# Expert results scattered to their nodes' rows and loaded in groups, in place of gathers; another graph's scatters moved earlier

## The chip, the cores and the metric

The kernel is one program on one core of a Trainium2 chip. Its engines run side by side, each through its own instructions in order: PE (matrix products), DVE (vector work), ACT (functions and copies), POOL (here mostly the issue of indirect DMAs, which gather or scatter rows by a list of indices) and SP (plain DMAs). ACT's queue issues some plain DMAs too. The metric is the device time of one execution in microseconds (us).

## The reference

A network of four pairs of layers on 3125 nodes with 256 values each. Every layer is added to x, and every layer but the first input sees a layer norm of x:

```python
x = x + L0_gnn(norm(x))   # sum over 100000 weighted edges
x = x + L0_ffn(norm(x))   # 8 experts of 512, the best 2 of each node
x = x + L1_gnn(norm(x))   # graph attention, two layers, 50000 edges
x = x + L1_ffn(norm(x))   # 8 experts, the best 2
x = x + L2_gnn(norm(x))   # weighted graph convolution, then two dense layers
x = x + L2_ffn(norm(x))   # 4 experts; the choice comes from attention over another graph, 65536 edges
x = x + L3_gnn(norm(x))   # two mean convolutions
x = x + L3_ffn(norm(x))   # 8 experts of 1024, the best 2
```

Three of these, L0_ffn, L1_ffn and L3_ffn, are what this document calls expert rounds:

```python
topk_vals, topk_idx = top_k(xf @ Wg + bg, 2)
w = softmax(topk_vals)
for e in range(8):
    out += w_of(e)[:, None] * (act(xf @ W1[e] + b1[e]) @ W2[e] + b2[e])   # w_of(e) is 0 for nodes that didn't choose e
```

## The kernel before

Nodes lie in 25 tiles of 128 (the last holds 53); x stays in SBUF as `X`. Tiles are treated in six groups: five tiles four times, then four, then one (`GROUPS`). The program runs its steps in turn: `r0_gnn`, taking up of edges, then `middle` (`r0_ffn`, `r1_gnn`, `r1_ffn`, in which POOL keeps the order of the program text), `r2_gnn`, `r2_ffn`, `r3_gnn`, `r3_ffn`.

**An expert round.** While the layer before is still running, `mix_group` takes each finished group: norm, router, the two best experts of each node, and the node's place among the rows of each of the two. `mix_send` (L869) then has POOL scatter the normalised rows, one indirect DMA for a tile and a choice, into `regions`, a DRAM table with a stretch for each expert: 50 a round. Two row buffers hold the groups that wait for this. `gated` works on what was sent, in chunks of 256 rows of one expert. 28 chunks are always run; some more stand behind a branch that the data here does not take. For a chunk, SP reads the expert's number and the row from SBUF into registers and issues four loads (`gx_xs`, 256 KB of rows, L987; `gx_w1`, `gx_w2`, `gx_b2`). PE transposes the rows, DVE copies them (`gx_xt`, L999), PE computes the first layer (L1004), ACT applies the function (L1005), and PE the second layer (`second`, L974), one chunk behind the first. DVE adds the bias for each half of the chunk (L976) into `gx_ys`, and ACT's queue stores the chunk's 256 KB to `ff_results` in the order of the chunks (L977). The loop's tiles in SBUF have two buffers each.

**The collection.** When all chunks are done, the branch is passed (its `settle` reads one row of the other graph's table, `os_mark`, L1838), and `mix_result` gathers, for each tile and each of the two choices, 128 result rows of 1 KB with an indirect DMA on POOL (`gb_y`, L360) and adds them to `X` with their weights on DVE (L1035): 50 gathers and 50 additions a round. The first collection runs inside the start of `r1_gnn`, the second inside that of `r2_gnn`, mixed with norms and matrix products; the last is followed only by the stores of the output.

The plain DMAs of SP and ACT use eight semaphores in rotation, so that an issue waits for the DMA eight issues before it.

**The other graph.** The 65536 edges that `r2_ffn` needs are sorted by 512 scatters of 128 records each into `os_table` (`own_send`, L1826) on POOL. They depend on nothing but their records, and are spread over the earlier steps: 2 at each step of `r0_gnn`'s matrix loop (0 or 1 in its last part), each released by a step's ACT copy; 3 in each chunk of `r0_ffn`; 9 at each of four calls in the first attention layer of `r1_gnn` (`tail`); 3 or 4 in each chunk of `r1_ffn`; and what is left, 21, behind it, where `own_send()` stands between the first four gathers of the second collection and the others on POOL. In a chunk they stand ahead of the chunk's second layer.

## Time and profile before

| what | value |
|---|---|
| median of 10 runs | 5708.17 us (5701.96 to 5719.6) |
| the profiled execution | 5703.31 us |
| its span | 5701.4 us |
| mean granted clock of TensorE | 0.796 |
| busy of the span: PE, DVE, ACT, POOL | 64%, 50%, 38%, 37% |
| POOL: scatters to the other graph's table | 512, 551.1 us |
| POOL: scatters to the regions | 150, 148.3 us |
| POOL: gathers of results | 150, 153.4 us |

One profiled execution is shown as a page (busy times, the span in 40 slices, queues, the chain of work that ended last, the costliest groups of instructions), and its trace answers questions on a stretch, a tile or a line. In a line of a group, `a<-b` names what is written and read, `x150` counts; then come the busy time and the mean ns of one, and behind the second bar the time that the engine stood idle just before these instructions, with what ended most of it. `SPq` and `ACTq` are the queues' own instructions. A clock of 0.65 in a window is the mean of what the throttle granted in it. Stages lie in the span at: `r0_gnn` until about 780 us, `r0_ffn` 780 to 1005, the first collection and `r1_gnn` from there, `r1_ffn` 2840 to 3030, the second collection and `r2_gnn` from there, `r3_ffn` 5210 to 5630, the last collection to the end.

### The profile page before, as it was taken

To read this page: it belongs to the slowest core of one execution; us is meant where nothing else is said; L and a number is where in the kernel's file an instruction comes from. 1 tells how busy PE (TensorE), PEld (TensorE's weight loads), DVE (VectorE), ACT (ScalarE), POOL (GpSimd) and SP (SyncE) were. 2 spreads that over 40 slices of the span, in tenths; PEclk is the share of its full clock that TensorE was granted. 3 is DMA by queue.
4 is the path that set the end of the run, shared out by engine and by line. 5 is a ranking of instruction groups with operands and counts; after the bars stand their busy time and mean duration, and the time that the engine had idled before them with its cause. 6 is when DMAs were issued, how large, how long until landed. Compare 5 with 4: busy or idle time off the path is not lost. (4 is left out here: it accounts for less than half of the span.)

```text
span 5701.4 us, 66173 instructions
## 1 busy us (share of the span) xinstructions
PE 3631.1 (64%) x20909; PEld 2866.4 (50%) x20909; DVE 2854.3 (50%) x9396; ACT 2171.4 (38%) x5957; POOL 2108.9 (37%) x2107
## 2 busy tenths in 40 slices
PE   1499979324545324444573887554666699997994
PEld 1389858223333213333352676432433488886883
DVE  7978732434444335454524787524544787422112
ACT  2556432134554335445411797311222443111221
POOL 0766433455555455555357000245454000011003
PEclk9699979656666656666696998776777799997997
DMA  1722247333333133333163222211111011233554
GB/s 50 237 82 93 100 157 223 100 98 93 106 95 101 49 91 98 94 93 94 55 191 93 107 93 82 57 18 25 22 22 22 11 58 65 82 103 123 190 194 142
DMA packets 329439, 543.00 MB, mean 95 GB/s; under 512 B 69071, under 2 KB 242003, under 8 KB 325873
## 3 DMA queue, kind: packets, MB, share of 16 engines
q1 hardware_dynamic: 213430, 354.48, 18.9%
q0 software_dynamic: 84032, 154.27, 10.8%
q10 hardware_dynamic: 31610, 29.84, 1.6%
q8 instruction: 173, 2.83, 0.2%
q14 instruction: 194, 1.58, 0.1%
HBM read 393.49 MB, written 145.37 MB: 95 GB/s over the span
## 5 line engine op out<-in xcount | busy, mean ns | idle before, releaser
L360 POOL DMA_INDIRECT ad_rows<-r_rows,fa_gi x832 | 831.4, 999 | 632.9 <-PE ad_acc L2223 339.1
L1826 POOL DMA_INDIRECT os_table<-os_rec,os_at x512 | 551.1, 1076 | 637.9 <-ACT gx_h L1005 186.0
L360 POOL DMA_INDIRECT ad_rows<-q_rows,own_gi x416 | 399.8, 961 | 877.6 <-DVE ad_hb L2104 506.9
L2213 ACT ACTIVATE ad_rows<-ad_rows 128x64 f32<-128x64 f32 x2544 | 640.3, 335 | 149.0 <-issue 146.4
L2223 PE MATMUL ad_acc<-ad_rows,ad_hd 128*128 128x260 f32 x1664 | 601.1, 523 | 33.5 <-ACT ad_rows L2213 27.9
L2223 PEld LDWEIGHTS ad_acc<-ad_rows,ad_hd 128*128 128x128 f32 x1664 | 417.3, 265 | 122.3 <-ACT ad_rows L2213 35.7
L1654 PE MATMUL r_pa<-r_xs,r_cnt 128*128 128x257 bf16 (+1 forms) x3750 | 459.8, 276 | 11.9 <-issue 11.7
L869 POOL DMA_INDIRECT regions<-gh_xn,gd_at x150 | 148.3, 989 | 844.3 <-PE r_pa L1654 545.3
L1005 ACT ACTIVATE gx_h<-gx_pa,gx_bias 128x256 f32<-128x256 f32 x392 | 184.9, 473 | 607.3 <-PE gx_pa L1004 547.2
L1654 PEld LDWEIGHTS <-r_cnt 128*128 128x128 bf16 x3750 | 364.8, 99 | 67.6 <-issue 16.7
L1004 PE MATMUL gx_pa<-gx_xt,gx_w 128*128 128x256 f32 x1568 | 371.0, 392 | 22.7 <-DVE gx_xt L999 18.7
L974 PE MATMUL gx_po<-gx_w,gx_h 128*128 128x256 f32 x1568 | 370.5, 382 | 9.9 <-ACT gx_h L1005 6.8
L976 DVE TENSOR_TENSOR gx_ys<-gx_po,gx_b 128x256 f32<-128x256 f32 x168 | 70.5, 423 | 566.8 <-PE gx_po L974 491.8
L1004 PEld LDWEIGHTS gx_pa<-gx_xt,gx_w 128*128 128x128 f32 x1568 | 298.3, 195 | 89.1 <-DVE gx_xt L999 35.8
L360 POOL DMA_INDIRECT gb_y<-ff_results,gd_at x150 | 153.4, 1023 | 487.0 <-SPq L126 437.5
L974 PEld LDWEIGHTS gx_po<-gx_w,gx_h 128*128 128x128 f32 x1568 | 291.8, 191 | 52.3 <-ACT gx_h L1005 10.5
L1521 PE MATMUL r_pa<-r_xn,r_wt 128*128 128x257 f32 x1250 | 303.1, 387 | 17.6 <-ACT r_wt L1557 17.2
L2126 PE MATMUL ad_pt<-ident,ad_e 128*4 128x128 f32 x75 | 26.1, 348 | 452.0 <-DVE ad_e L2123 204.7
L2112 ACT CAST ad_hd<-ad_hb 128x2176 f32<-128x2176 bf16 (+1 forms) x50 | 98.3, 1967 | 566.0 <-PE ad_acc L2223 426.3
L2600 PE MATMUL ss_sum<-r_xw,ss_wt 128*128 128x256 f32 x1250 | 289.8, 394 | 6.4 <-DMA ss_wt<-mats 6.4
L2182 PE MATMUL ad_px<-ad_nb,ad_hT 128*128 128x24 bf16 x1248 | 45.3, 180 | 354.5 <-DVE ad_nb L1420 265.5
L2600 PEld LDWEIGHTS ss_sum<-r_xw,ss_wt 128*128 128x128 f32 x1250 | 245.6, 198 | 41.7 <-issue 6.8
(573 smaller groups left out, 7189.8 us busy)
## 6 DMA issues: line engine op xcount, KB each, us to landing
gx_w<-in_L_ffn_W SPq DMA_DIRECT2D x56, 1024.0 KB
mats<-r_wt SPq DMA_DIRECT2D x25, 1600.0 KB
ss_wt<-mats SPq DMA_DIRECT2D x25, 1600.0 KB
gx_w<-in_L_ffn_W SPq DMA_DIRECT2D x56, 512.0 KB
regions<-zero SPq DMA_DIRECT2D x26, 1024.0 KB
ad_rb<-fa_relT SPq DMA_DIRECT2D x48, 544.0 KB
gx_xs<-regions SPq DMA_DIRECT2D x84, 256.0 KB
ff_results<-gx_ys ACTq DMA_DIRECT2D x84, 256.0 KB
```

Of the source, the lines that this page charges most:

```text
L360: return self.nc.gpsimd.indirect_dma_start(out=out, out_offset=None, in_=table[:, :], in_offset=bass.IndirectOffsetOnAxis(ap=idx, axis=0))
L869: ins = nc.gpsimd.indirect_dma_start(out=self.regions[:, :], out_offset=bass.IndirectOffsetOnAxis(ap=m.at[i][:, t:t + 1], axis=0), in_=x, ...
L974: nc.tensor.matmul(po, h[:, f, j * P:(j + 1) * P], w2s[:, f, :], start=f == 0, stop=f == FC - 1)
L1004: nc.tensor.matmul(ps, w1s[:, c, f * P:(f + 1) * P], xt[:, c, :], start=c == 0, stop=c == DC - 1)
L1005: done = nc.scalar.activation(h[:, f, :], ps, act, bias=bias1[:, f, k:k + 1])
L1521: nc.tensor.matmul(pa, wt[:, i, :], xn[:, g * G + i, :], start=i == 0, stop=i == G - 1)
L1654: nc.tensor.matmul(pa[:, 0:n], c[:, u, :], xs[i][:, u, j, 0:n], start=u == 0 and j == 0, stop=u == T - 1 and j == 2)
L1826: i = nc.gpsimd.indirect_dma_start(out=s.table[:, :], out_offset=bass.IndirectOffsetOnAxis(ap=s.at[:, c:c + 1], axis=0), in_=s.rec[:, c, : ...
L2112: nc.scalar.copy(x.hd[:, :x.kb, :], x.hb[:, :x.kb, :])
L2213: i = nc.scalar.activation(v, v, AF.Copy, scale=x.rt[:, k, W4 + h:W4 + h + 1])
L2223: nc.tensor.matmul(x.acc, lhs[:, k, :], rhs[:, k, :], start=i == 0, stop=i == x.kb - 1)
L2600: nc.tensor.matmul(sums[t], wt[:, d, :], xw[:, d, :], start=d == 0, stop=d == T - 1)
```

## The change

A row in the regions gets one value more, a code: the node's number, plus 4096 times the number of its first choice, plus a tag of the round. The region table, its clearing, the row buffers and `gx_xs` are 257 values wide. `mix_group` computes the code with three more DVE operations a group.

In a chunk, `places` reads the code column of the 256 rows and computes with seven DVE operations on 128x2 values where each result goes: row node of `ff_results` if the chunk's expert is the node's first choice, row 4096 + node if it is not, and a row beyond the table, which is dropped, if the row holds no node of this round. `second` scatters each half of the chunk with an indirect DMA on POOL (56 a round), in place of ACT's store. `results` has a fixed size and is allocated once a round at its start; the padding rows are cleared by two DMAs, and the round's clearing of 1 MB goes, as do the operations at the start of `gated` that computed where to gather.

`mix_results` loads a group of tiles for one choice by one plain DMA on SP (12 a round, up to three groups ahead, four buffers) and keeps the 50 additions. `settle` reads one value of the results, which waits for all of the round's scatters; it is called ahead of the branch, at the end of its body and behind it.

`own_send` is spread otherwise: 3 in place of 2 at each step of `r0_gnn`'s loop, 7 in place of 9 in `tail`, 1 in place of 3 or 4 in each chunk of `r1_ffn`, after which nothing is left for the call behind it.

The diff, without the places where only a width or a name follows from the above:

```diff
-        self.regions = self.dram.tile([8 * RC, D], F32, name="regions")
+        self.regions = self.dram.tile([8 * RC, D + 1], F32, name="regions")
...
     def settle(self):
-        pass
+        if self.landing is not None:
+            self.nc.sync.dma_start(self.landed, self.landing[0:1, 0:1])
...
         with self.tc.If(cond):
             yield
+            self.settle()
...
+        m.tag = pool.tile([P, T], F32, name="gd_tag")
+        nc.gpsimd.iota(m.tag, pattern=[[P, T]], base=TAG * m.n, channel_multiplier=1, allow_small_or_imprecise_dtypes=True)
+        m.far = pool.tile([P, E], F32, name="gd_far")
+        nc.gpsimd.iota(m.far, pattern=[[HALF, E]], base=0, channel_multiplier=0, allow_small_or_imprecise_dtypes=True)
+        m.results = self.dram.tile([2 * HALF, D], F32, name=f"ff{m.n}_results")
...
+        e1 = hp.tile([P, TG, E], F32, name="gh_e1")[:, :G, :]
+        nc.vector.tensor_tensor(e1, s1, m.far[:, None, :].to_broadcast(all_), OP.mult)
+        nc.vector.tensor_reduce(rows[:, :, D], e1, AX.X, OP.add)
+        nc.vector.tensor_add(rows[:, :, D], rows[:, :, D], m.tag[:, gs])
...
-            adj = pool.tile([P, E], F32, name="gd_adj")
-            nc.vector.tensor_sub(adj, end, nch)
-            nc.vector.scalar_tensor_tensor(adj, adj, float(CH), zero, op0=OP.mult, op1=OP.subtract)
+            self.landing = results
             for i in range(2):
-                q = pool.tile([P, T, E], F32, name="gd_q")
-                nc.vector.tensor_tensor(q, sel[i], adj[:, None, :].to_broadcast([P, T, E]), OP.mult)
-                qs = pool.tile([P, T], F32, name="gd_qs")
-                nc.vector.tensor_reduce(qs, q, AX.X, OP.add)
-                nc.vector.tensor_add(pos[i], pos[i], qs)
-                nc.vector.tensor_scalar_min(at[i], pos[i], float(K * CH - 1))
-            results = self.dram.tile([K * CH, D], F32, name=f"ff{n}_results")
+                nc.scalar.dma_start(results[i * HALF + N:i * HALF + NP, :], self.zero[0:NP - N, 0:D])
...
                         nc.vector.tensor_add(y[:, j, :], po, b2s)
-                    nc.scalar.dma_start(results[k * CH:(k + 1) * CH, :].rearrange("(j p) d -> p j d", p=P), y)
+                        i = nc.gpsimd.indirect_dma_start(
+                            out=results[:, :], out_offset=bass.IndirectOffsetOnAxis(ap=to[:, j:j + 1], axis=0),
+                            in_=y[:, j, :], in_offset=None, bounds_check=2 * HALF - 1, oob_is_err=False)
+                        tc.declare_no_dep(i.ins, group=f"ff{m.n}_results", reason="nodes are distinct")
+                        tc.add_to_no_dep_group(f"ff{m.n}_results", i.ins)
+
+                def places(k, xs):
+                    code = xs[:, :, D]
+                    ci_ = yp.tile([P, CJ], I32, name="gx_ci")
+                    nc.vector.tensor_scalar(ci_, code, float(-TAG * m.n), None, op0=OP.add)
+                    old = yp.tile([P, CJ], F32, name="gx_old")
+                    nc.vector.tensor_scalar(old, code, float(TAG * m.n), 4.0 * HALF, op0=OP.is_lt, op1=OP.mult)
+                    e = yp.tile([P, CJ], I32, name="gx_e")
+                    nc.vector.tensor_scalar(e, ci_, 12, None, op0=OP.arith_shift_right)
+                    half = yp.tile([P, CJ], F32, name="gx_half")
+                    nc.vector.tensor_scalar(half, e, ek[:, k:k + 1], float(HALF), op0=OP.not_equal, op1=OP.mult)
+                    nc.vector.tensor_scalar(ci_, ci_, HALF - 1, None, op0=OP.bitwise_and)
+                    nc.vector.tensor_add(half, half, old)
+                    to = yp.tile([P, CJ], I32, name="gx_to")
+                    nc.vector.tensor_tensor(to, half, ci_, OP.add)
+                    return to
...
-                        xs = xp.tile([P, CJ, D], F32, name="gx_xs")
+                        xs = xp.tile([P, CJ, D + 1], F32, name="gx_xs")
...
                         nc.vector.tensor_copy(xt, pt)
+                        to = places(k, xs)
...
-                        if k == 3:
-
-                            nc.scalar.dma_start(results[KA * CH:K * CH, :].rearrange("(q p) d -> p q d", p=P),
-                                                self.zero[:, None, 0:D].to_broadcast([P, (K - KA) * CJ, D]))
...
                 with self.branch(n > KA):
                     chunks(KA, K)
-        m.results = results
+        self.settle()
+        self.landing = None
...
-    def mix_result(self, m, pool, t):
-
-        nc = self.nc
-        for i in range(2):
-            y = pool.tile([P, D], F32, name="gb_y")
-            self.gather(y, m.results, m.at[i][:, t:t + 1])
-            nc.vector.scalar_tensor_tensor(self.X[:, t, :], y, m.w[i][:, t:t + 1], self.X[:, t, :], op0=OP.mult, op1=OP.add)
+    def mix_results(self, m, pool):
+        nc, ys = self.nc, []
+        groups = list(GROUPS)
+        def fetch():
+            g, n = groups.pop(0)
+            y = pool.tile([P, 2, TG, D], F32, name="gb_y")
+            for i in range(2):
+                nc.sync.dma_start(y[:, i, 0:n, :], m.results[i * HALF + g * P:i * HALF + (g + n) * P, :].rearrange("(t p) d -> p t d", p=P))
+            ys.append(y)
+        for g, n in GROUPS:
+            while groups and len(ys) < 3:
+                fetch()
+            y = ys.pop(0)
+            for t in range(n):
+                for i in range(2):
+                    nc.vector.scalar_tensor_tensor(self.X[:, g + t, :], y[:, i, t, :], m.w[i][:, g + t:g + t + 1],
+                                                   self.X[:, g + t, :], op0=OP.mult, op1=OP.add)
+            yield g, n
...
-                    self.own_send(2 if g < T // G - 1 else src % 2, done)
+                    self.own_send(3 if g < T // G - 1 else src % 2, done)
...
     def settle(self):
+        super().settle()
         self.nc.sync.dma_start(self.o.mark, self.o.table[0:1, :])
...
             def tail(i):
-                self.own_send(9, i)
+                self.own_send(7, i)
...
-        self.gated(self.mix, "L1_ffn_w1", "L1_ffn_b1", "L1_ffn_w2", "L1_ffn_b2", AF.Gelu, send=3, more=2, tail=False)
+        self.gated(self.mix, "L1_ffn_w1", "L1_ffn_b1", "L1_ffn_w2", "L1_ffn_b2", AF.Gelu, send=1, tail=False)
```

## The prediction

> **What bounds the kernel now.** I read the page's costliest groups first, for the price of each operation that the change touches, then the windows, because the kernel is a row of stages with different limits, then who waits for the gathers, and last the chain.
>
> ```profile
> L1826 POOL DMA_INDIRECT os_table<-os_rec,os_at x512 | 551.1, 1076 | 637.9 <-ACT gx_h L1005 186.0
> L869 POOL DMA_INDIRECT regions<-gh_xn,gd_at x150 | 148.3, 989 | 844.3 <-PE r_pa L1654 545.3
> L976 DVE TENSOR_TENSOR gx_ys<-gx_po,gx_b 128x256 f32<-128x256 f32 x168 | 70.5, 423 | 566.8 <-PE gx_po L974 491.8
> L360 POOL DMA_INDIRECT gb_y<-ff_results,gd_at x150 | 153.4, 1023 | 487.0 <-SPq L126 437.5
> ```
>
> An indirect DMA holds POOL for about 0.97 us, whether it gathers or scatters, and the timeline adds 0.30 us of issue: 1.28 us each.
>
> The windows (columns: us, busy us and count of PE, PEld, DVE, ACT, POOL, then clock, DMA share, GB/s):
>
> ```profile
> 332.00:612.00 280.00, 275.38 (x1832) 250.56 (x1832) 232.25 (x599) 168.47 (x481) 167.31 (x159) 1.00 0.26 92
> 612.00:660.00 48.00, 47.88 (x300) 43.51 (x299) 42.90 (x159) 23.51 (x52) 6.55 (x7) 1.00 0.24 90
> 660.00:780.00 120.00, 76.08 (x389) 63.80 (x387) 65.61 (x324) 46.45 (x93) 55.54 (x56) 0.72 0.27 95
> 780.00:1005.00 225.00, 217.10 (x1029) 180.89 (x1029) 51.56 (x116) 55.01 (x113) 81.59 (x84) 0.98 0.71 219
> 1005.00:1120.00 115.00, 42.58 (x152) 30.82 (x152) 67.55 (x202) 25.59 (x63) 52.95 (x53) 0.65 0.37 101
> 2840.00:3030.00 190.00, 134.05 (x564) 100.34 (x564) 47.29 (x120) 28.48 (x58) 96.65 (x101) 0.90 0.60 176
> 3030.00:3065.00 35.00, 0.00 (x0) 0.00 (x0) 4.71 (x22) 0.23 (x1) 24.64 (x26) 0.51 0.21 46
> 3065.00:3165.00 100.00, 44.25 (x149) 32.32 (x150) 77.28 (x155) 26.91 (x67) 69.90 (x71) 0.68 0.24 63
> 5210.00:5630.00 420.00, 409.07 (x1911) 352.51 (x1910) 44.05 (x90) 106.01 (x224) 0.00 (x0) 0.98 0.56 184
> 5630.00:5702.00 72.00, 0.00 (x0) 0.00 (x0) 24.03 (x50) 0.00 (x0) 47.54 (x50) 0.50 0.46 137
> ```
>
> 332 to 660 is the first graph layer: PE is full, and POOL's 159 sends leave it idle for part of the time. 780, 2840 and 5210 begin the three expert rounds of 28 chunks: the first and third are PE's (217 of 225, 409 of 420), the second nobody's (PE 134 of 190). The windows that begin at 1005, 3030 with 3065, and 5630 are those in which results are collected: there PE stands at 0 to 44%. In the last, POOL's 50 gathers at 1.28 us are 64 us of the 72, while DVE has 24 us to do.
>
> ```profile
> L360 POOL DMA_INDIRECT gb_y<-ff_results,gd_at x150: 942/946/2159, 1007.0 to 5691.6; - x150
>   SPq L126: 437.5, 3
>   DMA gb_y<-ff_results,gd_at: 103.1, 70
> ```
>
> DVE waits 103 us for gathers, in 70 pieces. In the second collection the timeline shows why most: four gathers, then 21 sends in a row on POOL, then the next gather, while DVE stands still for 25 us:
>
> ```profile
> 3037.79 1.00 POOL L1826 DMA_INDIRECT os_table<-os_rec,os_at  x1 [0.30 <-issue]
> ...
> 3064.66 0.98 POOL L360 DMA_INDIRECT gb_y<-ff_results,gd_at  x1 [0.30 <-issue]
> ...
> 3067.60 0.48 DVE L1035 SCALAR_TENSOR_TENSOR X<-gb_y,gd_w,X 128x256 f32<-128x256 f32 x1 [24.97 <-DMA gb_y<-ff_results,gd_at]
> ```
>
> The end, from 5630, is one chain of gather, landing and DVE operation; a short and a long landing from it:
>
> ```profile
> 5657.73 2.47 DMA gb_y<-ff_results,gd_at
> ...
> 5677.81 4.19 DMA gb_y<-ff_results,gd_at
> ```
>
> **The change part by part**, against the profiled span of 5701.4 us (its execution 5703.3; the median of the runs is 4.9 us above that).
>
> *The end, from 5630.* 50 gathers go, 12 plain loads on SP take their place: 6.5 MB. In the first expert round the DMA engines reach 300 to 350 GB/s for stretches, so they need 19 to 22 us, against DVE's 24. Before: last add 5624.4, first gather 5630.1. After: the last scatter is issued at 5624.5, lands by 5628 (as the gathers' 2.5 to 4.2 us), then the new read that waits for it, the branch, and the read again, some 2.2 us each (the read of this kind that is there already took 2.1, from 3030.2 until SP went on at 3032.3): loads from about 5636, first group there at 5640, the last of DVE's 50 operations at 5665. From its last one to the end it was 5.8 us; I keep that: 5671, or −30. The four big output stores compete with the loads: 9.7 MB at 300 GB/s from 5636 end at 5668, so they fit. Ends: −35 (a faster settling) and −20 (loads at the 219 GB/s of the first round's mean, 30 us, with the stores behind).
>
> *The second collection, 3032 to 3165.* Off POOL: 50 gathers and 21 sends, 91 us; 25 additions of 0.83 us stay. What is late next is DVE: 4.7 + 77.3 = 82 us of work in 133. With 8 us until the first group is there and DVE nine tenths busy the stage lasts about 100: −33. Ends −45 (DVE without a gap) and −20 (only the 27 us of the sends, less settling).
>
> *The first collection, 1005 to 1120.* DVE has 68 us, and POOL's gathers run from 1007.0 to 1079.8. Loading hides that, but the next layer's first gather, at 1119.6, waits for normalisation, transposes and DVE work that stay; and the two reads cost some 4 us. I take −10, ends −20 and 0.
>
> *Tail of the first attention.* There the sends, 9 a call, run on POOL in two bursts of 18 without a pause (1910 to 1933, 1944 to 1967), and the next gathers start at once at 1967.6. 7 for 9 in the two calls of the later burst: 4 × 1.28 = −5.
>
> *The first graph layer.* 3 sends a step for 2 moves about 100 sends in front of 660. A step takes 3.5 us; 3 × 1.28 = 3.8 exceed it. From 332 to 612 POOL was idle between sends for 280 − 159 × 1.28 = 77 us, room for 60 of the extra ones; 40 remain at 612, 51 us of POOL. Until 660 there are another 39 us of room. So the first group's region scatters (661.8 to 674.7), which stand behind the sends in POOL's order, are 12 to 30 us late. Behind them waits the normalisation of the group after next, on ACT and DVE, since the rows have two buffers (ACT already waits 4.1 us for a region scatter). Later groups have pauses of 15 us between them, which take up part: +10, ends 0 and +25. PE's matmuls up to 660 do not wait for POOL.
>
> [...]
>
> *The chunk loops.* Each chunk gains two scatters on POOL (2.6 us, with the sends 6.4 us in the first round's 8.0 us chunk, 3.8 in the second's 6.8, 2.6 in the third's 15.0), seven tiny DVE operations (0.15 to 0.19 us, as the small ones in the trace, 1.2 us), and a row of 1028 bytes; it loses ACT's store and its place in the eight semaphore lanes that SP's loads wait for. The last tiny operation reuses a buffer that both scatters of two chunks ago read, so DVE now waits for their landing, and behind it stands the next chunk's bias addition. In the first and third round the landing (4 us) fits in the chunk: 0, ends −5 and +10. In the second the PE part is only 4.8 us and SP's six issues and their waits set the pace; the freed lane gains up to 0.5 us a chunk (SP's stalls there were 0.7), the wait costs up to 0.9: 0, ends −15 and +25. The rows of 1028 bytes: packets of 1040 bytes take 47 to 55 ns in this trace, of 1024 bytes 46, in loops that DMA does not bound: nothing.
>
> [...]
>
> *Small things.* Three more DVE operations per group (18 × 0.19 a round), about ten fewer at each round's start, two of them 128x200: +1. The zero fill of 1 MB becomes 150 KB: nothing, since it was hidden.
>
> Sum: −30 − 33 − 10 − 5 + 10 + 0 + 0 + 1 = −67. 5703.3 − 67 = 5636; with the 4.9 us to the median, 5641.
>
> **The rivals.**
> *Slower: the scatters' landing paces the loops.* If DVE's seven operations and the wait for both scatters fall on the path, each chunk pays 1.2 us plus some of the 2.5 to 4.2 us. It decides from 67 / 84 = 0.8 us a chunk over all rounds; at 1.2 us in all 84 it is +101, 5742. For it: the order on DVE puts the wait ahead of the addition that frees PE's output. Against: in 56 chunks DVE is busy under 25% and PE has two output buffers.
> *The backlog eats half.* Regions come 30 us late or more and the second round pays its 25: −67 + 15 + 25 = −27, 5681. For it: POOL's three sends exceed a step. Against: 39 us of room after 612.
> *More.* The second round was bound by lanes and POOL's 101 scatters, and loses 15 us or more, and the second collection gives 45: −67 − 15 − 12 = −94, 5614. For it: nobody is full there. Against: DMA is at 0.60.
> *The loads bring little,* because the two reads and the branch eat the early start and DVE was the next limit anyway: ends at −20, −20, 0: −34, 5674.
>
> **How the numbers follow.** Forecast 0.45, backlog 0.15, little from loads 0.12, more 0.10, landing paces 0.18, of which three quarters or so end slower. Its own range is 5625 to 5660. 0.2% (11 us) is about what a measurement tells from no change. Faster 0.81, same 0.05, slower 0.14. The range from 5600 to 5706 leaves out the worst of the landing case and a few in 100 below.
>
> **What would show it.** Right: no gathers after 5630 and the span's end 30 us after the first load; DVE without the 25 us wait after 3030; the regions' first scatter at 675 to 690; chunk loops of 225, 190 and 420 us as before. Wrong: DVE waiting for a scatter's landing at the line that computes the destinations, PE idle on the additions, the second loop over 200 us; or the first round starting 30 us late.

## The result and the profile after

The changed kernel takes 5748.72 us (median of 8 runs, 5741.27 to 5760.29) against 5706.28 us before (28 runs): a ratio of 1.0074, 95% interval 1.0065 to 1.0083. It is slower by 42 us where 67 us less were forecast, and outside the range. The profiled execution took 5743.91 us, its span 5742.0 us at a mean TensorE clock of 0.797 (before: 0.796).

Cut at the same instructions in both traces, the span goes as follows (us; the first stage ends with the last matrix product of `r0_gnn`'s loop, a round runs from its first transposition to its last bias addition, the attention from its first gather to its last):

| stage | before | after | difference | forecast |
|---|---|---|---|---|
| until the end of the first graph layer's loop | 737.9 | 878.7 | +140.8 | +10 |
| to the first expert round | 47.5 | 59.4 | +11.9 | 0 |
| first expert round | 217.2 | 244.9 | +27.7 | 0 |
| first collection | 117.0 | 93.3 | −23.7 | −10 |
| attention | 1621.5 | 1608.0 | −13.5 | −5 |
| to the second round | 110.9 | 109.8 | −1.1 | 0 |
| second round | 174.2 | 162.7 | −11.5 | 0 |
| second collection | 145.8 | 95.2 | −50.6 | −33 |
| to the third round | 2042.7 | 2039.5 | −3.2 | 0 |
| third round | 409.8 | 410.2 | +0.4 | 0 |
| end | 77.0 | 40.3 | −36.7 | −30 |
| sum | 5701.4 | 5742.0 | +40.6 | −68 |

(The forecast had 1 us more for small things.)

So the gains came, and were larger than forecast: the three collections gave 111 us where 73 were expected. What was forecast at +10 cost 141, and the first round 28 more. The 11.9 us between the loop and the first round belong to the rows of 257 values: every kernel here that has them takes 55 to 62 us there, every one with rows of 256 takes 47.5 to 51.6. Which part of it costs this was not taken apart.

The windows of after that answer to those of before (columns as there: us, busy us and count of PE, PEld, DVE, ACT, POOL, then clock, DMA share, GB/s):

```profile
332.00:612.00 280.00, 235.97 (x1362) 204.42 (x1363) 172.63 (x436) 132.72 (x372) 188.10 (x176) 0.90 0.20 71
612.00:740.00 128.00, 108.40 (x606) 91.13 (x605) 76.96 (x198) 55.97 (x162) 82.63 (x78) 0.90 0.20 71
740.00:880.00 140.00, 122.01 (x725) 107.55 (x723) 95.99 (x364) 58.56 (x129) 58.10 (x57) 0.93 0.29 104
935.00:1190.00 255.00, 224.10 (x1016) 184.54 (x1014) 67.12 (x304) 53.39 (x113) 136.11 (x140) 0.96 0.63 190
1190.00:1280.00 90.00, 37.79 (x152) 27.98 (x152) 66.80 (x202) 25.38 (x63) 3.31 (x7) 0.71 0.43 132
2985.00:3150.00 165.00, 125.64 (x547) 95.39 (x548) 64.15 (x294) 26.74 (x55) 74.83 (x77) 0.92 0.65 191
3150.00:3245.00 95.00, 44.78 (x167) 32.84 (x166) 77.89 (x190) 32.38 (x77) 26.07 (x31) 0.73 0.31 92
5702.00:5742.00 40.00, 0.00 (x0) 0.00 (x0) 19.97 (x50) 0.00 (x0) 0.97 (x1) 0.55 0.75 247
```

In the last line nothing but DVE and the loads is left of the end, and in the second collection (3150) POOL is down to 26 us and DVE at 78 of 95: both as the prediction says. The surprise is in the first two lines. From 332 to 612 PE was busy 275 of 280 us before, at full clock; now 236, at 0.90, though no matrix product of this stage waits for anything that POOL writes. And POOL, which was expected to be full, issued 176 operations in 280 us, only 17 more than before.

The groups of after that belong to this, from the page's costliest:

```profile
L1872 POOL DMA_INDIRECT os_table<-os_rec,os_at x512 | 550.7, 1076 | 628.9 <-ACT gx_h L1040 154.1
...
L888 POOL DMA_INDIRECT regions<-gh_xn,gd_at x150 | 148.2, 988 | 847.1 <-PE r_pa L1700 544.8
...
L1567 PE MATMUL r_pa<-r_xn,r_wt 128*128 128x257 f32 x1250 | 334.9, 414 | 87.9 <-ACT r_wt L1603 53.3
...
L990 POOL DMA_INDIRECT ff_results<-gx_ys,gx_to x168 | 163.5, 973 | 406.6 <-DVE gx_ys L989 373.7
```

The 168 scatters of results hold POOL 0.97 us each, the 150 gathers 1.02. The loop's matrix product r_pa has a mean of 414 ns and 88 us of idle time before it. By windows, before's group from 332 to 612 and after's from 332 to 740:

```profile
L1521 PE MATMUL r_pa<-r_xn,r_wt 128*128 128x257 f32 x785 | 184.4, 380 | 3.5 <-ACT r_wt L1557 3.1 <-issue 0.4
```

```profile
L1567 PE MATMUL r_pa<-r_xn,r_wt 128*128 128x257 f32 x843 | 227.3, 416 | 60.1 <-ACT r_wt L1603 30.2 <-ACT r_degs L1569 20.9 <-issue 8.2
```

The tile of collected results in after, and the end as the timeline shows it on SP and on DVE:

```profile
L1079 DVE SCALAR_TENSOR_TENSOR X<-gb_y,gd_w,X x150: 377/475/1023, 1198.3 to 5734.3; 128x256 f32<-128x256 f32 x150
L1070 SPq DMA_DIRECT2D gb_y<-ff_results x36: 332/1450/2487, 1191.6 to 5724.9; - x36
its engine sat idle before it (us, times) until:
  DMA gb_y<-ff_results: 15.0, 4
```

```profile
5706.76 2.15 SPq L112 DMA_DIRECT2D landed<-ff_results  x2
...
5709.45 15.91 SPq L1070 DMA_DIRECT2D gb_y<-ff_results  x12
```

```profile
5701.31 0.42 DVE L989 TENSOR_TENSOR gx_ys<-gx_po,gx_b 128x256 f32<-128x256 f32 x1 [3.03 <-PE gx_po L987]
5714.80 20.00 DVE L1079 SCALAR_TENSOR_TENSOR X<-gb_y,gd_w,X 128x256 f32<-128x256 f32 x50 [13.06 <-DMA gb_y<-ff_results]
```

DVE's wait for collected results fell from 103 us to 15. At the end, last bias addition, reads, loads and the first result addition follow in 13 us, and the 50 additions then run without a gap in 20.0 us.

PE's stalls in the first graph layer look like this in after's timeline (PE and ACT; a bracket gives the idle time before an instruction and what ended it):

```profile
703.82 0.97 POOL L1872 DMA_INDIRECT os_table<-os_rec,os_at  x1 [0.30 <-issue]
704.64 0.27 PE L1599 MATMUL r_pw<-r_hs,r_hd 128*128 128x128 f32 x1 [0.66 <-issue]
705.10 0.97 POOL L1872 DMA_INDIRECT os_table<-os_rec,os_at  x1 [0.30 <-issue]
705.38 0.27 PE L1599 MATMUL r_pw<-r_hs,r_hd 128*128 128x128 f32 x1 [0.47 <-issue]
706.09 1.12 PE L1567 MATMUL r_pa<-r_xn,r_wt 128*128 128x257 f32 x4 [0.45 <-issue]
...
709.64 0.81 PE L1567 MATMUL r_pa<-r_xn,r_wt 128*128 128x257 f32 x3 [1.20 <-issue]
711.09 0.27 PE L1599 MATMUL r_pw<-r_hs,r_hd 128*128 128x128 f32 x1 [0.64 <-issue]
```

In the middle of a row of matrix products whose operands are all there, PE pauses again and again for 0.3 to 1.2 us that the trace puts down to no wait at all ("issue"), while POOL issues one send after the other. POOL's row of sends ends at 709.9 (its next one starts at 714.27, after 4.38 us without one), and PE's last pause ends at 711.79.

### The profile page after: what moved, and what is told of

It reads as the page before. It is cut to its first block, busy times and chain, and to the rows that moved or that the text cites. A ratio compares the mean times of both kernels' runs of the same rounds, so it can differ in the third digit from the quotient of the medians.

```text
span 5742.0 us, 66747 instructions
## 1 busy us (share of the span) xinstructions
PE 3674.1 (64%) x20909; PEld 2889.5 (50%) x20909; DVE 2912.2 (51%) x10008; ACT 2169.5 (38%) x5957; POOL 2121.0 (37%) x2131
## 3 DMA queue, kind: packets, MB, share of 16 engines
q0 software_dynamic: 84896, 153.90, 10.4%
## 5 line engine op out<-in xcount | busy, mean ns | idle before, releaser
L1872 POOL DMA_INDIRECT os_table<-os_rec,os_at x512 | 550.7, 1076 | 628.9 <-ACT gx_h L1040 154.1
L1700 PE MATMUL r_pa<-r_xs,r_cnt 128*128 128x257 bf16 (+1 forms) x3750 | 458.8, 276 | 12.0 <-issue 11.9
L1567 PE MATMUL r_pa<-r_xn,r_wt 128*128 128x257 f32 x1250 | 334.9, 414 | 87.9 <-ACT r_wt L1603 53.3
L1567 PEld LDWEIGHTS r_pa<-r_xn,r_wt 128*128 128x128 f32 x1250 | 245.3, 207 | 137.8 <-ACT r_wt L1603 81.8
L990 POOL DMA_INDIRECT ff_results<-gx_ys,gx_to x168 | 163.5, 973 | 406.6 <-DVE gx_ys L989 373.7
L2643 PEld LDWEIGHTS ss_sum<-r_xw,ss_wt 128*128 128x128 f32 x1250 | 244.0, 197 | 40.6 <-issue 6.7
```

The costliest lines, as they stand in the source:

```text
L990: i = nc.gpsimd.indirect_dma_start(out=results[:, :], out_offset=bass.IndirectOffsetOnAxis(ap=to[:, j:j + 1], axis=0), in_=y[:, j, :], in_ ...
L1567: nc.tensor.matmul(pa, wt[:, i, :], xn[:, g * G + i, :], start=i == 0, stop=i == G - 1)
L1700: nc.tensor.matmul(pa[:, 0:n], c[:, u, :], xs[i][:, u, j, 0:n], start=u == 0 and j == 0, stop=u == T - 1 and j == 2)
L1872: i = nc.gpsimd.indirect_dma_start(out=s.table[:, :], out_offset=bass.IndirectOffsetOnAxis(ap=s.at[:, c:c + 1], axis=0), in_=s.rec[:, c, : ...
L2643: nc.tensor.matmul(sums[t], wt[:, d, :], xw[:, d, :], start=d == 0, stop=d == T - 1)
```

## The experiments

Two parts of the change were suspected of the first 141 us: the third send per step, and the rows of 1028 bytes, of which the regions' clearing has 26624. For the first round there was the prediction's own rival, the wait for the scatters' landing. The runs went to four chips. Those named with chip 1 and chip 4 met a before of 4867 and 4865 us, those with chip 5 and chip 6 one of 5694 to 5698 and 5646 us; the result above belongs with the second kind by its time. Each ratio below is against before on the same chip, and stages are compared within one kind of chip.

### Sends, clearing, buffers and the third send by itself, on chip 1

The changed kernel with the sends spread as before:

```diff
-                    self.own_send(3 if g < T // G - 1 else src % 2, done)
+                    self.own_send(2 if g < T // G - 1 else src % 2, done)
...
-                self.own_send(7, i)
+                self.own_send(9, i)
...
-  AF.Gelu, send=1, tail=False)
+  AF.Gelu, send=3, more=2, tail=False)
```

> The changed kernel with the sends spread as before (2 a step in the first graph layer, 9 in the attention's tail, 3 or 4 a chunk in the second round, 21 behind it). Theory: the third send a step keeps POOL running longer than a step and holds up PE; the loop of matrix products, which ran from 241 to 879 us in place of 241 to 738, ends some 85 us earlier, at about 795, and the rest of its delay, some 55 us, stays with the clearing. Against that the later places pay again: 13 us in the attention, 11 in the second round, 30 to 50 in the second collection, so 5690 to 5725 in all. Rival: the layer is late because of the clearing alone, the sends are hidden: the loop still ends at about 879, and the time is 5790 to 5820.

The changed kernel with the regions cleared in runs of 832 bytes instead of rows of 1028:

```diff
-        v = self.regions.rearrange("(q p r) d -> q p r d", p=P, r=8)
-        for q in range(v.shape[0]):
-            self.nc.sync.dma_start(v[q], self.zero[:, None, 0:D + 1].to_broadcast([P, 8, D + 1]))
+        v = self.regions.rearrange("(p r) d -> p (r d)", p=P).rearrange("p (c e) -> p c e", e=208)
+        for q in range(0, v.shape[1], 10):
+            n = min(10, v.shape[1] - q)
+            self.nc.sync.dma_start(v[:, q:q + n, :], self.zero[:, None, 0:208].to_broadcast([P, n, 208]))
```

> The changed kernel, the same bytes of the regions cleared in runs of 832 bytes, each at a multiple of 64 bytes, in place of rows of 1028. Theory: writes of 1028 bytes at addresses that are no multiple of 64 cost 94 ns a packet against 51 for 1024; with 832 aligned bytes a packet takes 40 to 50 ns, the clearing ends by 275 us as before, and the time falls by 45 to 60 us, to about 5695. Rival: the packets are slow since more traffic runs beside them; then 832 bytes take as long, and the time stays within 10 us of 5748.

The changed kernel with four buffers for the tiles of a chunk's results and destinations:

```diff
-tc.tile_pool(name="gx_y", bufs=2) as yp
+tc.tile_pool(name="gx_y", bufs=4) as yp
```

> The changed kernel with four buffers in place of two for the results and their destinations in the chunk loop, so that DVE waits for the scatters of four chunks ago. Theory: in the first round the wait for the landing goes (149 us of DVE's waits in 26 pieces), PE no longer waits for the additions, and the round takes 217 us as before in place of 245: the time falls by 25 to 30 us, to about 5720. Rival: the seven small DVE operations and the scatters on POOL themselves cost the 28 us: no change, within 8 us of 5748.

And the kernel before with the third send alone:

```diff
-                    self.own_send(2 if g < T // G - 1 else src % 2, done)
+                    self.own_send(3 if g < T // G - 1 else src % 2, done)
```

> The kernel before with 3 sends a step in the first graph layer and nothing else changed; what is sent there is missing from the end, so the second round sends fewer and nothing is left behind it. Theory: PE stalls as in the changed kernel, the loop of matrix products ends 70 to 100 us later than at 738; the second collection saves its 27 us and more: 5745 to 5780. Rival: the sends are hidden where POOL was idle: loop at 738 to 750, the time 5660 to 5685.

Measured, with stages in us:

| kernel | median | ratio and interval | loop ends | first round | second round | second collection |
|---|---|---|---|---|---|---|
| e1_sends_back | 4910.30 | 1.0093 (1.0077 to 1.0110) | 737.8 | 240.7 | 208.1 | 106.2 |
| e2_aligned | 4868.45 | 1.0002 (0.9992 to 1.0011) | 760.5 | 245.0 | 168.0 | 94.5 |
| e3_bufs4 | 4829.98 | 0.9928 (0.9911 to 0.9944) | 770.6 | 217.3 | 133.4 | 100.6 |
| e5_before_send3 | 4901.15 | 1.0070 (1.0054 to 1.0087) | 770.2 | 216.9 | 139.8 | 115.7 |

A run on chip 4 that sends and clears as fast as before does (e8_again, below) ends the loop at 700.1, so the third send costs 70 us of the loop here, and it does so as the prediction had described it: not by PE's stalls, but by the backlog on POOL. The windows of e5_before_send3:

```profile
332.00:612.00 280.00, 280.00 (x1862) 256.31 (x1861) 242.11 (x641) 166.54 (x472) 222.33 (x190) 1.00 0.27 97
612.00:700.00 88.00, 50.37 (x323) 45.37 (x321) 43.38 (x152) 25.81 (x56) 67.94 (x66) 0.81 0.16 52
```

and of e8_again, with two sends a step:

```profile
332.00:612.00 280.00, 280.00 (x1862) 256.30 (x1861) 241.78 (x641) 166.50 (x473) 165.00 (x159) 1.00 0.27 97
612.00:700.00 88.00, 84.05 (x520) 75.11 (x518) 69.76 (x266) 51.00 (x108) 36.24 (x36) 0.96 0.33 121
```

Until 612 PE is full in both, to the matrix product. But POOL got through 190 sends only: 222 us busy and 190 × 0.30 = 57 us of issue fill all of the 280. A send held it 1.17 us on average, with the issue 1.47, not 1.28; with two sends a step the mean was 1.04 (165.0 / 159). Why it rises is not shown. After 612 it had sends alone to do until the first scatter to the regions at 710.8 (645.5 in e8_again), and PE stands still for it once, in e5_before_send3's timeline:

```profile
730.41 1.22 PE L1521 MATMUL r_pa<-r_xn,r_wt 128*128 128x257 f32 x2 [67.81 <-ACT r_wt L1557]
```

That is ACT's copy queued behind a normalisation that waits for the regions' scatter (ACT's `gh_xn` waits for such scatters 4 times in that run, 82.3 us in all). Of the 70 us the second collection gave back 32 (147.6 to 115.7), and 34 stand in the total.

The landing wait is real in the first round, and four buffers remove it here: 245 to 217 us, which is before's time, and 168 to 133 in the second round. In after's first round the list of DVE's waits has

```profile
DVE gx_to L1010 <- DMA ff_results<-gx_ys,gx_to: 149.3, 26, 7.7
DVE gx_ys L989 <- PE gx_po L987: 7.6, 5, 4.5
```

(us in all, times, longest), and in e3_bufs4's the first line is gone; DVE now waits for the chunk's rows instead, in a round that PE fills:

```profile
DVE gx_ci L1000 <- DMA gx_xs<-regions: 115.0, 24, 5.7
DVE gx_ys L989 <- PE gx_po L987: 19.7, 22, 4.7
```

On this chip the change with four buffers is faster than before, with its three sends and its slow clearing.

### The same things on chip 5

The changed kernel again; the kernel before with the third send (the same kernel as e5_before_send3); the changed kernel with the aligned clearing (as e2_aligned); and all three repairs in one (aligned clearing, four buffers, sends as before).

> The changed kernel again, beside the runs that undo parts of it, since chips differ (on one the kernel before takes 5706 us, on another 4867). On the first: 1.0074 of the kernel before, the loop of the first graph layer ends at 879 us. On the second, from the runs that undo one part each: 4880 to 4920, 1.003 to 1.010 of the kernel before; the loop ends at 765 to 785 us without stalls of PE; the clearing's packets take 84 ns; the first round 245 us, the second 165 to 175.

> The kernel before with 3 sends a step in the first graph layer, again. On a chip on which the kernel before takes 5706 us: theory, PE stalls after some ten sends without a pause and the loop ends 70 to 100 us later than at 738 (5745 to 5780 in all); rival, the stalls of the changed kernel came from the clearing or the wide rows, and the loop ends at 738 to 775. On a chip like the last one: 1.007 again.

> The changed kernel with the clearing in aligned runs of 832 bytes and nothing else, on a chip of the kind on which the change was measured. Theory: the third send a step sets the first layer there, so the clearing is worth only the 20 us by which the changed kernel's loop (879) ends behind that of the kernel before with 3 sends (859): loop at 850 to 865, the time 15 to 25 us below the changed kernel's, 1.003 to 1.005 of the kernel before. Rival: its full length, 45 to 60 us: 0.996 to 0.999.

> The changed kernel with all three mended: aligned clearing, four buffers for results and destinations, sends spread as before. Theory: the loss in the first graph layer and the first round is gone and the gains in the collections stay: 1.5 to 2.3% faster than the kernel before on either chip (5575 to 5620, or 4755 to 4795). Rival: the second collection's gain came from having no sends behind the second round; then it is 0.8 to 1.2% faster at most.

| kernel | median | ratio and interval | loop ends | first round | second round | second collection |
|---|---|---|---|---|---|---|
| n_after | 5736.66 | 1.0078 (1.0053 to 1.0104) | 878.3 | 246.2 | 159.2 | 95.0 |
| e5_again | 5749.44 | 1.0096 (1.0064 to 1.0128) | 858.9 | 218.2 | 144.2 | 114.8 |
| f2_aligned | 5718.11 | 1.0034 (1.0019 to 1.0048) | 854.3 | 245.8 | 162.8 | 95.1 |
| e4_all | 5699.55 | 1.0004 (0.9990 to 1.0019) | 740.4 | 252.9 | 234.3 | 105.1 |

The result repeats. The third send alone moves the loop's end by 121 us (737.9 to 858.9), not by 70 as on chip 1. The aligned clearing takes 24 us off the changed kernel's loop (878.3 to 854.3). With both undone the loop is back at 740.4. The clearing itself, in after and then in f2_aligned (times of one issue, minimum, median and maximum in ns, and first and last start):

```profile
L104 SPq DMA_DIRECT2D regions<-zero x26: 539/5398/6810, 182.5 to 309.8; - x26
```

```profile
L105 SPq DMA_DIRECT2D regions<-zero x26: 372/3293/4148, 182.3 to 260.4; - x26
```

Before's last one starts at 264.7. Of the packets in the trace, those of 1028 bytes took 94 ns on average, before's of 1024 bytes 51 ns, f2_aligned's of 832 bytes 44 ns. PE feels it: from 180 to 332 it is busy 57 us in after and 92 in before, and one copy r_wt of ACT waits 20.3 us, until 334.8, for a store of the matrices that SP issued behind the clearing, at 323.3. On chip 1, where the sends do not stall PE, e1_sends_back shows the clearing by itself: its loop ends at 737.8, e8_again's on chip 4 at 700.1.

How far the loop is at a given time tells where its delay arises. It has 1250 products r_pa; the ends of three of them, in us:

| kernel | chip | 125th | 1125th | 1250th |
|---|---|---|---|---|
| before | of the result | 291.4 | 659.5 | 737.9 |
| after | of the result | 345.7 | 807.4 | 878.7 |
| e5_again | 5 | 318.9 | 780.2 | 858.9 |
| f2_aligned | 5 | 288.7 | 783.3 | 854.3 |
| e8_again | 4 | 292.7 | 643.4 | 700.1 |
| e5_before_send3 | 1 | 292.3 | 643.5 | 770.2 |

On the result's kind of chip the whole delay is there by the 1125th product, and the first scatter to the regions follows it within 3 us (809.6 in after, 782.5 in e5_again), as in before (661.8): POOL's backlog has no part in it. On chip 1 nothing is lost by the 1125th, and all 70 us come after it, in the wait for the regions. So the third send costs the loop on both kinds of chip, but in two different ways.

e4_all shows the other side. With the sends back in the rounds and four buffers, the loop is repaired, but the second round takes 234 us: here POOL has 3 or 4 sends and two scatters a chunk. And the first round, which four buffers had brought to 217 us on chip 1, stays at 253.

### Where the sends can go, on chip 5

e7_mix is e4_all with 2 or 3 sends in turn at a step and 2 a chunk in the second round:

```diff
-                    self.own_send(2 if g < T // G - 1 else src % 2, done)
+                    self.own_send(2 + src % 2 if g < T // G - 1 else src % 2, done)
...
-  AF.Gelu, send=3, more=2, tail=False)
+  AF.Gelu, send=2, tail=False)
```

> As the last, with the sends spread in between: 2 and 3 by turns in the first graph layer, 9 in the tail, 2 a chunk in the second round, 15 behind it. Theory: 2.5 x 1.28 = 3.2 us fits in a step of 3.5, so the loop ends as before, and the second round loses less to sends than with 3 or 4: 0 to 15 us faster than the run with all three mended. Rival: what counts is that POOL pauses within a step; then the loop stalls or regions come late, and it is slower than that run by 20 us or more.

5709.63 us, 1.0025 (1.0014 to 1.0037): loop 792.9, first round 251.9, second round 194.5. Half of a third send is half of the cost (52 us), and the second round gets shorter with fewer sends (234.3 us with 3 or 4 a chunk, 194.5 with 2). f1_nosend0 is e4_all without the 84 sends of the first round, which then go behind the second:

```diff
-beside=self.fill_edges, send=3, tail=False
+beside=self.fill_edges, send=0, tail=False
```

> All three mended (aligned clearing, four buffers, sends as before), and no sends in the first round: its 84 are sent behind the second round, so only the first round is to be read. Theory: five indirect DMAs a chunk (6.4 us of POOL in 7.5) hold up the first round on chips of this kind, not the scatters of results as such; with two a chunk it takes 215 to 222 us as before the change, in place of 246 to 253. Rival: the new scheme itself (the wait for landing, the small operations on DVE) costs the 30 us: 240 or more.

One run, 5772.83 us, with the first round at 220.2 us: on this kind of chip, with four buffers, it is the sends beside the scatters that lengthen the round, and not the new scheme as such. With them POOL has 5 indirect DMAs in a chunk of 7.75 us (217 / 28), at 1.28 us each 6.4 of it. Two a chunk cost nothing, as in the third round, which takes 410 us with its 56 scatters and without. How five of them hold up the round is open: in e4_all's first round PE's 25 us of idle time all stand before instructions that carry a wait. The 84 sends behind the second round made that collection 189 us.

### What in a third send stops PE

Four variants of before. Three have one thing more at each of the 100 steps of the loop's four full groups: m1_poolwork adds POOL arithmetic of 0.77 us, m2_hwdma a small plain DMA on SP, and f4_few an indirect DMA of 16 single values to a table that nobody reads:

```diff
+                    if g < T // G - 1:
+                        x = nc.gpsimd.tensor_add(scr, scr, scr)
```

```diff
+                    if g < T // G - 1:
+                        x = nc.sync.dma_start(extra[g * T + src], self.o.rec[:, g * T + src, :])
```

```diff
+                    if g < T // G - 1:
+                        x = nc.gpsimd.indirect_dma_start(
+                            out=extra[:, :], out_offset=bass.IndirectOffsetOnAxis(ap=few[0:16, g * T + src:g * T + src + 1], axis=0),
+                            in_=scr[0:16, 0:1], in_offset=None, bounds_check=1600 - 1, oob_is_err=False)
```

m4_burst leaves the number of sends and puts them in rows of ten:

```diff
-                    self.own_send(2 if g < T // G - 1 else src % 2, done)
+                    self.own_send((10 if src % G == G - 1 else 0) if g < T // G - 1 else src % 2, done)
```

> The kernel before, with one addition of 128x288 on POOL more at each step of the first graph layer (100 of about 0.9 us, released like a send), so POOL is as busy as with 3 sends but issues no more DMAs; the output is the same. On a chip on which the kernel before takes some 5700 us: theory, PE is held up by the issue of indirect DMAs without a pause; the additions are hidden in POOL's idle time, the loop still ends at 738 to 765 us. [...] On a chip on which it takes some 4870 us: hidden, at most 10 us.

> The kernel before, with one plain DMA on SP more at each step of the first graph layer that writes 128 records of 4 bytes to a scratch table (100 in all, released like a send), so the DMA engines get the small writes of a third send while POOL issues none of them; the output is the same. Theory: what holds PE up is POOL's issuing, so the loop ends at 738 to 760. Rival: the small writes or their completions hold PE up: 820 to 870.

> The kernel before with the same number of sends in the first graph layer, but 10 at each fifth step in place of 2 at each. Theory: PE stalls when POOL has issued some ten indirect DMAs without a pause, so ten at once and 4 us of pause stay near that limit: loop at 738 to 770. Rival A, it is the number of sends that counts: 738 to 745. Rival B, what counts is any stretch in which POOL issues without a pause: later than 770.

> The kernel before with one indirect DMA of 16 records (in place of 128) more at each step of the first graph layer, to a scratch table; the output is the same. It takes POOL nearly the same issue as a whole send. Theory: what holds PE up is the number of indirect DMAs that POOL issues without a pause, so the loop ends at 820 to 860 as with 3 whole sends. Rival: it is the small writes, an eighth here: 740 to 765.

| kernel | chip | median | ratio and interval | loop ends |
|---|---|---|---|---|
| m1_poolwork | 6 | 5646.95 | 1.0002 (0.9985 to 1.0019) | 741.5 |
| m2_hwdma | 6 | 5676.69 | 1.0053 (1.0039 to 1.0068) | 764.0 |
| m4_burst | 6 | 5657.17 | 1.0014 (1.0002 to 1.0027) | 746.5 |
| f4_few | 5 | 5809.35 | 1.0195 (1.0169 to 1.0222) | 869.8 |

POOL's time is not the price: 76 such additions between 332 and 612, 59 us, cost nothing, though POOL is busy 243 of the 280 us there and only 188 in after. Nor are bytes or the table's random rows: 100 indirect DMAs of 64 bytes each cost the loop 132 us (869.8 against before's 737.9), somewhat more than 100 sends (121). Rows of ten sends alone cost little. Each indirect DMA beyond two a step costs the loop 1.0 to 1.3 us on these chips (52 us for 50 in e7_mix, 121 for 100 in e5_again, 132 for 100 in f4_few). The groups of f4_few between 332 and 740 (columns as in the page's groups; several releasers are given):

```profile
L1528 PE MATMUL r_pa<-r_xn,r_wt 128*128 128x257 f32 x852 | 226.7, 411 | 27.9 <-ACT r_wt L1564 14.0 <-issue 13.0
...
L1560 PE MATMUL r_pw<-r_hs,r_hd 128*128 128x128 f32 x851 | 123.3, 289 | 25.1 <-issue 20.9 <-DVE r_hs L1551 1.9 <-DVE r_hd L1556 1.9
```

More than half of the idle time before PE's matrix products ends with no wait. Sorted by whether the matrix product or its weight load carries a wait, and counted within the window from the modelled end of one to the start of the next, PE's idle time is:

| kernel | chip | window | at a wait, us | without one, us |
|---|---|---|---|---|
| before | of the result | 332 to 612 | 4.1 | 0.5 |
| after | of the result | 332 to 740 | 41.1 | 22.5 |
| e5_again | 5 | 332 to 740 | 55.8 | 19.2 |
| f4_few | 5 | 332 to 740 | 27.4 | 35.5 |
| m4_burst | 6 | 332 to 612 | 6.7 | 7.6 |
| m1_poolwork | 6 | 332 to 612 | 10.4 | 0.0 |
| e5_before_send3 | 1 | 332 to 640 | 0.0 | 0.0 |

The pauses without a wait stand at the end of long rows. Take as a row the indirect DMAs that POOL starts with less than 0.45 us between one and the next: of after's 40 such pauses of over 0.15 us, 38 begin at or behind the ninth DMA of a row, in f4_few 49 of 52, and in m4_burst all 15 between 332 and 612 at the tenth and last or just behind it. This is what m4_burst's expectation called the limit of some ten, and why its rows of ten cost little: each loses only its end. On chip 1 POOL runs on from 332 to 612 and PE has no such pause.

The waits are mostly for ACT's copy r_wt. That it comes late because PE's products before it were late is an inference; no run separates the two. In after the loop's rate falls from 785 products r_pa in 280 us (2.80 per us) to 843 in 408 (2.07), which is 107 us: 59 from PE's idle time (64 of 408 us instead of 5 of 280), and the other 49 from longer products, 416 ns instead of 380 for r_pa, at a granted clock of 0.90 instead of 1.00.

DVE is slower beside POOL's arithmetic: from 332 to 612 DVE's r_hd takes 486 ns in m1_poolwork and 366 in before. It is hidden all the same, since DVE at 274 of 280 us stays beside PE; and it is not what the sends do, beside which r_hd takes 366 ns in e5_again too.

### The part that pays, without the sends

e8_hybrid keeps 257 values a row (cleared in runs of 832 bytes) but uses the new scheme, scatters and group loads, in the third round only; the first two rounds store, gather and send as before. Its core, where `place` is true in the third round:

```diff
+        place = m.n == 3
...
-                        i = nc.gpsimd.indirect_dma_start(
+                        if not place:
+                            continue
+                        i = nc.gpsimd.indirect_dma_start(
...
+                    if not place:
+                        nc.scalar.dma_start(results[to * CH:(to + 1) * CH, :].rearrange("(j p) d -> p j d", p=P), y)
```

> Rows of 257 values with an aligned clearing, sends as in the kernel before, results scattered and loaded in the third round only (28 chunks of 15 us, 2 scatters each); the first two rounds store by chunk and gather as before. Theory: the gain of the last collection (77 us to 40) stays and nothing is lost: 5655 to 5675 where the kernel before takes 5700, 4825 to 4835 where it takes 4867, 0.992 to 0.9945 of it. Rival: the wider rows cost in the other places: 0.997 to 1.000.

On chip 6 5617.64 us against 5645.73, a ratio of 0.9944 (0.9925 to 0.9964): faster than before, where the changed kernel has 1.0074 and 1.0078. Loop 728.8, first round 217.6, second round 166.1, end 39.8. What the change brings at the end it keeps.

e9_hybrid4 adds one send a chunk in its second round, so that none is left behind it:

```diff
-  AF.Gelu, send=3, more=2, tail=False)
+  AF.Gelu, send=4, more=2, tail=False)
```

> The kernel with the new scheme in the third round alone, with 4 or 5 sends in each chunk of the second round in place of 3 or 4, so that none is left behind it. Theory: a send there costs some 0.4 us of the round (174 us with 98, 144 with about 20), and the 21 behind it 27 us of the collection: 12 to 20 us faster than with 3 or 4, 0.990 to 0.993 of the kernel before. Rival: more than four indirect DMAs a chunk hold up PE, the round takes 25 us longer, and nothing is won.

5660.69 us on chip 5, 0.9940 (0.9918 to 0.9962). The collection is 32 us shorter than e8_hybrid's (147.6 to 115.6) and the round 35 longer (166.1 to 201.5): nothing won. e10_late21 moves the call for the 21 left sends behind the collection in the program's text:

```diff
         self.gated(self.mix, "L1_ffn_w1", ..., send=3, more=2, tail=False)
-        self.own_send()
...
+            self.own_send()
             self.own_load()
```

> The same kernel as e8_hybrid, for the chip of this call, beside e10. Both theories: 28 us below before (0.994 to 0.996), second round 166 to 175 us, collection behind it 146 to 148 us, with DVE's wait of some 25 us behind the 21 sends.

> As e8_hybrid, but the 21 sends that are left stand behind the second collection's 50 gathers instead of behind its first four. Theory that DVE's 25 us wait for a gather queued behind the sends is time on the path: the collection's additions end some 20 us earlier, and of that 0 to 20 us are lost again where the other graph's table is read 27 us later; 10 to 20 us below e8_hybrid (0.9965 to 0.9985 of it, 0.990 to 0.992 of before). Rival, that POOL's 71 indirect DMAs in a row set the collection whatever their order: the same time as e8_hybrid, with the stage from the last addition of the second round to the first sums of the third layer at 146 to 148 us.

On chip 4 e8_again takes 4828.21 us, 0.9926 (0.9909 to 0.9943), and e10_late21 4825.46, 0.9919 (0.9903 to 0.9936): no difference between the two that these runs can tell. The edit did less than its expectation supposed: the scheduler put the sends among the gathers, from 2506.6 to 2571.0, and not behind the last. The gathers and result additions of the first two rounds in e8_again:

```profile
L369 POOL DMA_INDIRECT gb_y<-ff_rows,gd_at x100: 942/946/2265, 976.5 to 2583.4; - x100
L1092 DVE SCALAR_TENSOR_TENSOR X<-gb_y,gd_w,X x100: 437/479/1099, 981.2 to 2590.8; 128x256 f32<-128x256 f32 x100
```

and in e10_late21:

```profile
L369 POOL DMA_INDIRECT gb_y<-ff_rows,gd_at x100: 942/947/2262, 976.7 to 2584.7; - x100
L1092 DVE SCALAR_TENSOR_TENSOR X<-gb_y,gd_w,X x100: 444/480/1277, 981.3 to 2595.2; 128x256 f32<-128x256 f32 x100
```

The additions of the second collection begin 27 us earlier (2480.8 in place of 2507.9), yet the last gather starts 1 us later and the last addition 4 us later; the stage takes 148.6 us in place of 147.6. The list of DVE's waits between 2470 and 2600 has for e8_again

```profile
DVE X L1092 <- DMA gb_y<-ff_rows,gd_at: 40.3, 17, 24.0
```

and for e10_late21

```profile
DVE X L1092 <- DMA gb_y<-ff_rows,gd_at: 48.0, 28, 6.2
```

The one long wait became many short ones. POOL's 71 indirect DMAs stand with no pause of over 4 us in both, and as far as these two orders tell, their number sets the collection, not their order; e9_hybrid4, which has the 50 gathers alone there, shows what fewer are worth. The bare order, all sends behind all gathers, wasn't tried.

## Why the prediction was wrong

*The first graph layer: +10, bounds 0 and +25, measured +141.* This is the step that failed, in three places.

The sentence "PE's matmuls up to 660 do not wait for POOL" is true and did not help. On the result's kind of chip PE is slower beside long rows of indirect DMAs, in part by pauses without any wait, and before hardly shows it: with two sends a step POOL seldom has so long a row there (one of eight and one of ten between 250 and 612). e5_again, the third send alone, puts 121 us to this, the aligned run, 854.3 against 737.9, 116 us, and all of it by the 1125th product. The backlog, which was the whole of the forecast's +10, cost nothing here: the regions' first scatter came at 809.6, not at 675 to 690, because the loop was late and not POOL.

The price of a send was taken from the shortest cases of the timeline, 0.97 + 0.30 = 1.28 us, while the group's line, quoted at the head of the prediction, gives a mean of 1076 ns. On chip 1, where PE has no stalls and the backlog is all there is, a send took 1.47 us in this stage. So the 60 extra sends that were to fit until 612 were 31 (190 − 159); 69 were left instead of 40, and the regions' first scatter came 65 us late (710.8 to 645.5), not 12 to 30. The rule that followed, rows late by two buffers, ACT queued behind, was right; its size was 70 us. The mean of the stage alone would not have been enough: before's 1.05 + 0.30 us leaves room for 48 of the extra sends, and the price rose once POOL was full.

The rows of 1028 bytes were put at nothing, from packets of 1040 bytes that took 47 to 55 ns. Half of those 12800 packets were reads of DRAM and half stores to it (`r_rows<-hd_hx`, 50 of 130 KB), so that price told little of the 26 MB of the clearing, whose packets took 94 ns. With runs of 832 bytes at multiples of 64 the same clearing takes 44 ns a packet, so it is the length or the start of the rows and not the traffic beside them; which of the two is not shown. Worth 24 us on chip 5, and with two sends a step 38 (737.8 on chip 1 against 700.1 on chip 4). The wider rows also stand in the 11.9 us behind the loop, for which the sum had nothing.

*The chunk loops: 0, 0, 0, measured +27.7, −11.5, +0.4.* The first round's upper end was +10. The wait that was named is there, 149 us of it on DVE's line for the destinations, and "the landing (4 us) fits in the chunk" failed: with 3 sends between a chunk's scatters, landing and queue took up to 7.7 us of a chunk. Four buffers cure it on chip 1; on chip 5 the round with five indirect DMAs a chunk is still 36 us longer with four buffers (252.9 against 217.2), and only fewer of them bring 220 us. In the second round the 1 in place of 3 or 4 sends outweighs the two scatters. The third is right.

*The collections and the end: −10, −33, −30, measured −23.7, −50.6, −36.7.* Right in kind and place; each is a little beyond its good end (−20, −45, −35). For the end, the reads and loads took 13 us from the last bias addition where I had 16, and DVE's additions started 0.40 us apart where I had 0.50; the last part took 7 us where 5.8 were kept. For the second collection, "off POOL: 50 gathers and 21 sends" was the right reason, and DVE's wait of 25 us only its mark: e10_late21 breaks that wait up and gains nothing, e9_hybrid4 takes the sends out and gains 32 us there.

*The first attention's tail: −5, measured −13.5.* Kernels with the sends as before there have 1595 to 1622 us on chips 5 and 6 and in before's profile, so it can't be told from the spread of that stage.

*The rivals.* "The landing paces the loops" had the right place in the first round, 1 us a chunk, and not in the others; by itself it would not have made the kernel slower. That its 5742 us lies close to the measured 5748.72 is chance: the time was lost in the first graph layer, for which that rival kept +10. "The backlog eats half" was the mechanism on chip 1, at more than twice the price given, and not on the result's kind of chip. That the sends slow PE itself was not among the rivals. Of the signs of being wrong that the prediction listed, the wait for a scatter's landing came, and so did the late first round, by 153 us (938.1 against 785.3).

## What to carry to other kernels

A filler that has free time on its own engine need not be free: here the third sends moved the loop's end by 70 us on chip 1 and by 121 on chip 5. Price it by the mean of its group in the stage that it goes to, not by its shortest case, take that as a lower bound if it will fill its engine (a send held POOL 1.04 us with two a step and 1.17 with three), and then ask what it does to the engine that sets the pace, by a run with the filler alone in the old kernel: e5_before_send3 differs from before in one number, and would have shown the sign. A change of several parts is worth trying part by part; here one part, the group loads at the end, is worth 28 to 37 us, and the others together cost that and more.

## What the runs showed that was not expected

- On the result's chip and on chips 5 and 6 PE pauses beside indirect DMAs of POOL, without a wait, from the ninth or tenth of them in a row: 22.5 us in after between 332 and 740, 35.5 in f4_few, 7.6 in m4_burst between 332 and 612, against 0.5 in before. It goes with their number in a row and not with their bytes (64 bytes each in f4_few), and not with POOL being busy (m1_poolwork). On chip 1 the same kernel as e5_again has none. What inside the chip does this is open; no run here tells it.
- Chips differ by more than the change: before takes 4867 and 4865 us on chips 1 and 4, 5646 on 6, 5694 to 5698 on 5. The attention stage alone, with 832 gathers on POOL, is 1180 us in e8_again and 1604 in e8_hybrid, the same kernel. So a ratio holds for the kind of chip it was measured on: the changed kernel with four buffers is 0.9928 on chip 1, and with all repairs 1.0004 on chip 5.
- Small plain DMAs cost the loop as well: 100 of 512 bytes each moved its end from 741.5 us (m1_poolwork, same chip) to 764.0. Most of this is there by the 125th product r_pa (291.8 and 311.9), the stretch in which the regions are cleared; behind it the two loops keep nearly the same pace.
- Clearing DRAM in rows of 1028 bytes: 94 ns a packet (84 on chip 1), against 51 for 1024 and 44 for 832 bytes.
